# Pinning the norms, moving the choice of experts, and handing VectorE's work to ScalarE and GpSimd in the first third of a fused attention and mixture-of-experts block

## The chip, the cores and the metric

One core of a Trainium2 chip runs the whole program. The core has five engines, each with its own in-order instruction queue: TensorE (PE in the profile: matrix products and transposes), VectorE (DVE), ScalarE (ACT: activation functions and copies), GpSimd (POOL) and SyncE (SP, which mostly issues transfers). A queue starts its next instruction only when the one before it was started and its own waits are over, so what stands in front of what in a queue matters as much as how long it takes. The metric is the device time of one execution in microseconds (us). The kernel before has a median of 1208.85 us over five runs, from 1207.24 to 1213.85.

## The reference, cut to what matters

The input `x` holds 8 batches of 512 tokens with 512 features, in fp32.

```python
xn = layernorm(x)                                  # no weight, no bias
# attention: 16 heads of 32, chunks of 128 tokens, decayed linear attention
q = rotate(silu(xn @ Wq)); k = rotate(silu(xn @ Wk)); v = xn @ Wv
scores = einsum('bthd,bshd->bhts', q_c, k_c) * D   # D: decay mask of a chunk
o = scores @ v_c + (q_c * decay_q) @ S             # S: state carried over chunks
gate = xn @ Wg1 @ Wg2
o = group_rmsnorm(o * sigmoid(gate)) * norm_weight
s = o @ Wo
# mixture of experts: 16 experts of width 128, 4 chosen for each token, and a shared expert
logits = xn @ gate_w.T
weights, experts = top_k(softmax(logits), 4); weights /= weights.sum()
mixed = sum(weight_e * (silu(xn @ Wg[e]) * (xn @ Wu[e])) @ Wd[e])     # over the 4
shared = (silu(xn @ sWg) * (xn @ sWu)) @ sWd * sigmoid(xn @ shared_gate_w)
out = x + s * silu(mixed + shared)
```

## The kernel before, in words

The program is one long stretch of code for the core, with these stages (times in the span of the profiled execution):

- **0 to about 206 us.** The generator `first()` takes the 8 batches in turn. For each it makes the router's products (`route_1`: partial logits of all 512 tokens, four slices of the features side by side, copied to SBUF as `lT` by DVE, L311; `route_2`: their sum for each token, L323, then the four best experts, their weights and one-hot masks `oh` and `mask` on DVE), the shared expert (`share_1`: two products `pg` and `pu`, a SiLU on ACT, a product `h` on DVE, L366; `share_2`: four products `pys`, each of them taken out of PSUM and scaled by the shared gate `sg`, L380 on DVE or L382 on ACT, and stored to `sh_d`), the layer norm of the batch after next (`norm`: statistics L252 and L254 and centering L244 on DVE, the root of the variance on POOL, L256 and L258) and the transposes of the next batch (`turn`, L291, with ACT's copies L293). Each `yield` ends a piece. Beside these pieces runs the attention of batch 0: `value` (L576), `gate_1` to `gate_3` (L589, L598, L610), `enter` and `sequence` (rotated keys and queries L621, scores L679 and L700, outputs L718 and L722, root mean squares L729 to L754, projection L761). The function `along()` hands out 9 pieces of `first()` for every 5 of its steps.
- **206 to 246 us.** `sort()` gives each of the 16,384 pairs of token and expert a place in the list of its expert. Its long DVE steps are, for each of the four choices, a product `oa` (L445) and a sum over experts (L447), then small integer steps.
- **246 to 322 us.** `table()` turns the places into a table: which token stands at which row of which block of 128 rows. For each group of 16 lists, `make(i)` fills two one-hot arrays in fp16 on DVE, `place` (is the row equal to n: L512, then times the token's number: L514) and `block` (L517), in two halves of 8 lists each, and PE multiplies them into `pn` (L536). There are 8 groups. The generator is moved on by `between[0]`, which is called after every 4th of a product of `rotated` or `value`; beside it runs the attention of batch 1. Batch 1's own chain is on the same DVE.
- **340 to 740 us**: the expert blocks, each gathered, multiplied and stored. **745 to 1204 us**: the attention of batches 2 to 7 with the sum of everything. The change touches nothing there.

What sets the order: `on_pe()` chains every PE instruction behind the one traced before it, so PE's order is the order of the code. `behind(engine)` pins an instruction behind the last one traced for that engine. Everything without such a pin is placed by a scheduler that works out an order for each queue when the kernel is built. PSUM has 8 banks, given out in turn by tag: "a" has banks 0 to 3, "m" is bank 4, "d" is banks 5 and 6, "k" is bank 7. A matrix product must wait until the former holder of its bank has been read.

SP's queue holds, in the stretch of the sort and the table, the stores `s_d` of batch 0's projection (`spill`, L934), the loads `wexp` of 12 experts (L999, 768 KB each), stores of zeros (L1003) and the load of the transposed batch 2, `xT_2` (L558).

Of the kernel before, what the change touches and what calls it, by code (L numbers as in the profile page):

```python
# [11 lines left out]
F16 = mybir.dt.float16  # L12
# [7 lines left out]
P = 128  # L20
# [23 lines left out]
QUAD = 4  # L44
# [7 lines left out]
def shape_constants():  # L52

    f = np.float32
    c = {}
    lam = -(f(2.0) ** (f(-8.0) * (np.arange(H, dtype=f) + f(1.0)) / f(H))).astype(f)
    i = np.arange(C, dtype=f)
    diff = i[None, :] - i[:, None]
    dec = np.exp(lam[None, :, None] * np.maximum(diff, f(0.0))[:, None, :])
    c["dmask"] = np.where(diff[:, None, :] >= 0, dec, f(0.0))  # L60
    dq = np.exp(lam[:, None] * (i[None, :] + f(1.0)))
    c["dq"] = np.repeat(dq.reshape(G, HG, 1, C), HD, axis=2).reshape(G, P, C).transpose(1, 0, 2)
    c["dk"] = np.exp(lam[None, :] * (f(C) - f(1.0) - i[:, None]))
    lc = np.exp(lam * f(C))
    c["lamc"] = np.repeat(lc.reshape(G, HG, 1), HD, axis=2).reshape(G, P).T

    c["carry"] = np.tile(c["lamc"][:, :, None, None] * (np.arange(NC - 1) > 0), (1, 1, HD, 1))
    half = HD // 2
    theta = (f(BASE) ** (f(-2.0) * np.arange(half, dtype=f) / f(HD))).astype(f)
    ang = (np.arange(N, dtype=f)[None, :] * theta[:, None]).astype(f)  # L70
    c["cos"] = np.tile(np.cos(ang), (2 * HG, 1))
    c["sin"] = np.tile(np.concatenate([-np.sin(ang), np.sin(ang)], axis=0), (HG, 1))
    c["ident"] = np.eye(P)


    sel = np.zeros((P, H - HG + Q))
    exp = np.zeros((H, G, P))
    for g in range(G):
        for j in range(HG):
            sel[j * HD : (j + 1) * HD, H - HG + j] = 1.0 / HD  # L80
            exp[g * HG + j, g, j * HD : (j + 1) * HD] = 1.0
    c["sel"] = sel

    c["four"] = np.tile(np.eye(Q), (P // Q, P // Q))
    c["fold"] = np.tile(np.eye(Q)[:, :EA], (P // Q, 1))

    c["tri"] = np.triu(np.ones((P, P)), 1)
    c["iota_e"] = np.tile(np.arange(E), (P, 1))
    c["reset"] = np.tile((np.arange(NT) > 0)[None], (P, E)).reshape(P, E * NT)
    out = {k: np.ascontiguousarray(v.reshape(P, -1), dtype=f) for k, v in c.items()}  # L90
    out["exp"] = exp.reshape(H, D).astype(f)
    out["iota_b"] = (np.arange(P, dtype=f)[:, None] // Q * NBQ + np.arange(NBQ, dtype=f)).astype(f)

    out["whole"] = np.tile(np.arange(NB), (P, 1)).astype(np.float16)
    out["token"] = (
        np.arange(NT)[None, :] * P + np.arange(P)[:, None] - B * N // 2).astype(np.float16)
    return out


# [1 line left out]
def tile_block(ctx: ExitStack, tc: tile.TileContext, a: dict, out: bass.AP):  # L101
# [61 lines left out]
    iota_e = load(p1, "iota_e", [P, E])  # L163
    tri = load(p1, "tri", [P, P])
    reset = load(p1, "reset", [P, E * NT])
    token = load(const, "token", [P, NT], F16)
    whole = load(const, "whole", [P, NB], F16)
    iota_b = load(p1, "iota_b", [P, NBQ])
    ones = p1.tile([P, P], F32, tag="ones", name="ones")
# [62 lines left out]
    def norm(b):  # L232
        xs = xs_of[b]
        mv = p1.tile([P, NC, 2], F32, tag="mv", name=f"mv_{b}", bufs=2)
        rstd = p1.tile([P, NC], F32, tag="rstd", name=f"rstd_{b}", bufs=2)
        tiles = [slice(t, t + 1) for t in range(NC)] if b == 0 else [slice(0, NC)]

        def stand(engine):
            return behind(engine) if b < 2 else nullcontext()

        def center(ts):
            for t in range(ts.start, ts.stop):
                with stand(DVE):
                    nc.vector.tensor_scalar(  # L244
                        xs[:, t, :], xs[:, t, :], mv[:, t, 0:1], rstd[:, t : t + 1],
                        ALU.subtract, ALU.mult)

        for i, ts in enumerate(tiles):
            for t in range(ts.start, ts.stop):
                st = p1.tile([P, 6], F32, tag="st", name=f"st_{b}_{t}", bufs=4)  # L250
                with stand(DVE):
                    nc.vector.bn_stats(st, xs[:, t, :])  # L252
                with stand(DVE):
                    nc.vector.bn_aggr(mv[:, t, :], st)  # L254
            with stand(POOL):
                nc.gpsimd.tensor_scalar(rstd[:, ts], mv[:, ts, 1], LN_EPS, None, ALU.add)  # L256
            with stand(POOL):
                nc.gpsimd.tensor_tensor(  # L258
                    rstd[:, ts], rstd[:, ts],
                    root.to_broadcast([P, ts.stop - ts.start]), ALU.pow)  # L260
            if i:
                center(tiles[i - 1])
        center(tiles[-1])
        nc.sync.dma_start(
            xn_d[b * N : (b + 1) * N, :D].rearrange("(t p) d -> p t d", p=P),
            xs[:, :, : D // 2].bitcast(U16))
# [47 lines left out]
    def route_2(b):  # L314
# [9 lines left out]
        sg = p1.tile([P, NC], F32, tag="sg", name=f"sg_{b}", bufs=2)  # L324
        nc.scalar.activation(sg, lg[:, :, E], AF.Sigmoid)
        sg_of[b] = sg
        mx = p1.tile([P, NC, 8], F32, tag="mx", name=f"mx_{b}", bufs=2)
        ix = p1.tile([P, NC, 8], U32, tag="ix", name=f"ix_{b}", bufs=2)
        for t in range(NC):
# [39 lines left out]
    def share_2(b):  # L369
        h, sg = h1_of.pop(b), sg_of.pop(b)  # L370
        xT1_of.pop(b)
        for t in range(NC):
            sh = p1.tile([P, D], F32, tag="sh1", name=f"sh1_{b}_{t}", bufs=6)
            py = bank("dmaa"[t], f"pys_{b}_{t}")
            with on_pe():
                nc.tensor.matmul(
                    py, lhsT=h[:, t * P : (t + 1) * P], rhs=sw[:, KC * 2 * F :],
                    start=True, stop=True)
            if t % 2:
                nc.vector.tensor_scalar(sh, py, sg[:, t : t + 1], None, ALU.mult)  # L380
            else:
                nc.scalar.activation(sh, py, AF.Copy, scale=sg[:, t : t + 1])  # L382
            nc.sync.dma_start(sh_d[b][t * P : (t + 1) * P, :], sh)


    def sort():
# [54 lines left out]
        pos = p1.tile([P, TOPK, NT], F32, tag="pos", name="pos")  # L441
        bl = p1.tile([P, 2, TOPK, NT], I32, tag="bl", name="bl")
        for r in range(TOPK):
            with behind(DVE):
                nc.vector.tensor_tensor(oa[:, r], oh[:, r], at, ALU.mult)  # L445
            with behind(DVE):
                nc.vector.tensor_reduce(  # L447
                    pos[:, r], oa[:, r].rearrange("p e t -> p t e"), axis=AX.X, op=ALU.add)
            with behind(DVE):
                nc.vector.tensor_copy(posi[:, r], pos[:, r])  # L450
            with behind(DVE):
                nc.vector.tensor_scalar(bl[:, 0, r], posi[:, r], P - 1, None, ALU.bitwise_and)
            with behind(DVE):
                nc.vector.tensor_scalar(bl[:, 1, r], posi[:, r], 7, None, ALU.logical_shift_right)
            with behind(DVE):
                nc.vector.tensor_copy(
                    sp.rearrange("p w (r t) -> p w r t", t=NT)[:, :, r], bl[:, :, r])
            yield
# [16 lines left out]
    def table(room):  # L475
# [16 lines left out]
        free[0] = WE * LATE  # L492
        homes.append((part(quads, P, QUAD), part(quads, NB, QUAD)))
        count = part(NB, QUAD)
        acc = room[:, free[0] // 2 :][:, :NB]
        nc.scalar.copy(count, whole.unsqueeze(2).to_broadcast([P, NB, QUAD]))

# [4 lines left out]
        def make(i):  # L502
            place, block = homes[i // GROUP % 2]
            for u in range(0, quads, 2):
                us = slice(u, u + 2)
                lists = slice(i + u * QUAD, i + (u + 2) * QUAD)
                first = lists.start % NT

                def counts(n):
                    return count[:, :n].unsqueeze(1).to_broadcast([P, 2, n, QUAD])  # L510

                nc.vector.tensor_tensor(  # L512
                    place[:, us], counts(P), rows(sp[:, 0, lists], P), ALU.is_equal)
                nc.vector.tensor_tensor(  # L514
                    place[:, us], place[:, us], rows(token[:, first : first + 2 * QUAD], P),
                    ALU.mult)
                nc.vector.tensor_tensor(  # L517
                    block[:, us], counts(NB), rows(sp[:, 1, lists], NB), ALU.is_equal)

        make(0)  # L520
        for _ in range(KC + 1):
            yield
        for i in range(0, TOPK * NT, GROUP):
            if i + GROUP < TOPK * NT:
                make(i + GROUP)
            else:
                for e in range(E - LATE, E - LATE // 2):
                    nc.sync.dma_start(wexp[:, e, :], a["experts"][:, e, :])
# [4 lines left out]
            for some in ((0, 5), (5, 10), (10, GROUP)):  # L533
                with on_pe():
                    for j in range(*some):
                        nc.tensor.matmul(  # L536
                            pn[:, :NB], lhsT=place[:, j // QUAD, :, j % QUAD],
                            rhs=block[:, j // QUAD, :, j % QUAD], start=(j == 0),
                            stop=(j == GROUP - 1))
                if some[1] == GROUP:  # L540
                    if i:
                        nc.vector.tensor_tensor(acc, acc, pn[:, :NB], ALU.add)
# [394 lines left out]
    def first():  # L937

        for b in range(B):
            if 0 < b < B - 1:  # L940
                halves(b + 1)
            route_1(b)
            yield
            share_1(b)
            yield
# [8 lines left out]
            yield  # L954
            share_2(b)
            yield
        next(sorting)

    sorting = sort()
# [20 lines left out]

    for t in range(NC):
        value(0, t)
        along()
    gate_1(0)
    gate_2(0)
    gate_3(0)
    along()
    enter(0, along)
    sequence(0, along, spill, also=lambda: next(sorting, None))
# [324 lines left out]
```

## Time and profile before

| | us |
|---|---|
| median of five runs | 1208.85 (1207.24 to 1213.85) |
| the profiled execution | 1205.38 |
| its span | 1203.6 |
| PE busy in the span | 1160.5 (96%) |
| DVE busy | 751.9 (62%) |
| POOL busy | 437.9 (36%) |
| ACT busy | 407.2 (34%) |

The profiled execution is 3.47 us faster than the median and faster than each of the five runs. All durations below are from it. The mean clock that TensorE was granted is 0.993 of full speed.

How to read it: PE is busy for 96% of the span, so time is gained only where PE stops, where its clock is lowered, or where it does less. The 43 us in which PE stands still are 23.5 us before 340 us and less behind; the list of PE's waits says which engine and which line ended each of them. Shares of busy time of the other engines are averages over stages; what counts is whether DVE or ACT is the one that PE waits for in a given stretch.

### The profile page before, as it was taken

How to read it: one execution, taken by the hardware profiler on the slowest of the kernel's cores; microseconds unless marked ns; L12 is line 12 of the kernel's file. 1: busy time of each engine (PE TensorE's matmuls, PEld its weight loads, DVE VectorE, ACT ScalarE, POOL GpSimd, SP SyncE). 2: the span in 40 equal slices, each digit the busy share in tenths (PEclk: the TensorE clock that was granted, in tenths of full speed). 3: DMA queues.
4: the chain of work that ended last, by engine and by line, in shares of the span. 5: the costliest groups of instructions: out<-in, count | busy, mean ns of one | idle time of the engine just before them, and what ended most of it. 6: DMA issues, size and time to landing. Idle time of an engine off the chain costs nothing. (4 is left out here: it accounts for less than half of the span.)

```text
span 1203.6 us, 21260 instructions
## 1 busy us (share of the span) xinstructions
PE 1160.5 (96%) x7708; PEld 684.3 (57%) x7708; DVE 751.9 (62%) x1584; ACT 407.2 (34%) x767; POOL 437.9 (36%) x424
## 2 busy tenths in 40 slices
PE   6999999999999999999999999999999999999997
PEld 3435554446557777777777775545544545545453
DVE  6387554889414444444434444979879599598784
ACT  3343333320274444444444442141141411411420
POOL 3123002100213333333333331862876847858111
PEclk9999999989999999999999999999999999999999
DMA  9884231183458999989999996931845627544012
GB/s 325 286 296 166 102 136 71 25 315 117 146 150 212 224 233 229 227 229 231 229 213 234 223 222 186 344 119 56 271 130 182 206 87 252 146 125 145 18 39 68
DMA packets 163496, 217.16 MB, mean 180 GB/s; under 512 B 89792, under 2 KB 98880, under 8 KB 161472
## 3 DMA queue, kind: packets, MB, share of 16 engines
q1 hardware_dynamic: 141984, 143.88, 40.0%
q0 software_dynamic: 21120, 70.34, 21.1%
q10 hardware_dynamic: 288, 1.57, 0.4%
q8 instruction: 64, 1.05, 0.4%
q14 instruction: 40, 0.33, 0.1%
HBM read 125.55 MB, written 72.35 MB: 164 GB/s over the span
## 5 line engine op out<-in xcount | busy, mean ns | idle before, releaser
L1076 PE MATMUL pgu<-wexp,xt 128*128 x1088 | 257.6, 380 | 1.5 <-ACT xt L1057 1.2
L1076 PEld LDWEIGHTS pgu<-wexp,xt 128*128 128x128 f32 x1088 | 206.0, 190 | 88.6 <-issue 31.1
L1035 POOL DMA_INDIRECT xg<-xn_d,slot x79 | 74.6, 944 | 249.3 <-DVE y L1106 164.1
L1173 POOL DMA_INDIRECT yg<-y_d,posi x128 | 140.4, 1097 | 47.2 <-SPq L1140 19.6
L1081 DVE TENSOR_TENSOR slb<-slb,pgu 128x128 f32<-128x128 f32 x136 | 39.0, 287 | 189.6 <-ACT slb L1080 189.6
L1059 ACT COPY xt<-pl 128x512 uint16<-128x512 uint16 x136 | 104.3, 767 | 131.4 <-DMA pl<-xg 75.9
L1097 PE MATMUL py<-wexp,hT 128*128 x272 | 139.3, 594 | 0.1
L576 PE MATMUL pv<-wv,xT 128*128 128x512 f32 x256 | 119.9, 604 | 3.9 <-DVE sh L380 2.8
L621 PE MATMUL pk<-xT,wk 128*128 128x512 f32 x256 | 118.3, 603 | 1.7 <-DVEq L1140 1.7
L621 PE MATMUL pq<-xT,wq 128*128 128x512 f32 x256 | 117.4, 599 | 0.0
L761 PE MATMUL pw<-wo,on 128*128 128x512 f32 x224 | 102.3, 604 | 3.1 <-DVE m L1201 3.0
L1205 POOL TENSOR_TENSOR xo<-xo,m 128x512 f32<-128x512 f32 x30 | 43.2, 1440 | 152.1 <-DVE m L1201 142.3
L1035 POOL DMA_INDIRECT more<-xn_d,slot x57 | 53.6, 941 | 109.5 <-DVE y L1106 106.6
L700 DVE TENSOR_TENSOR sc<-ps,dmask 128x512 f32<-128x512 f32 x128 | 79.1, 676 | 0.8 <-PE ps L679 0.8
L576 PEld LDWEIGHTS pv<-wv,xT 128*128 128x128 f32 x256 | 45.7, 191 | 58.1 <-issue 51.3
L621 PEld LDWEIGHTS pq<-xT,wq 128*128 128x128 f32 x256 | 47.8, 193 | 52.8 <-issue 51.5
L1106 DVE TENSOR_SCALAR y<-py,xg 128x512 f32<-128x512 f32 x79 | 59.3, 750 | 29.2 <-PE py L1097 29.1
L621 PEld LDWEIGHTS pk<-xT,wk 128*128 128x128 f32 x256 | 46.1, 190 | 52.0 <-issue 49.6
L761 PEld LDWEIGHTS pw<-wo,on 128*128 128x128 f32 x224 | 41.8, 192 | 54.5 <-issue 47.0
L1080 ACT ACTIVATE slb<-pgu 128x128 f32<-128x128 f32 x136 | 37.8, 278 | 85.6 <-PE pgu L1076 85.3
L626 ACT ACTIVATE sk<-pk 128x512 f32<-128x512 f32 x32 | 19.1, 596 | 116.4 <-PE pk L621 107.6
L580 ACT COPY v<-pv 128x512 f32<-128x512 f32 x32 | 18.8, 589 | 108.3 <-PE pv L576 102.5
(169 smaller groups left out, 1765.1 us busy)
## 6 DMA issues: line engine op xcount, KB each, us to landing
y_d<-y SPq DMA_DIRECT2D x136, 256.0 KB, 3.0
wexp<-in_experts SPq DMA_DIRECT2D x14, 768.0 KB, 11.5
sh_d<-sh SPq DMA_DIRECT2D x32, 256.0 KB, 2.7
m<-sh_d SPq DMA_DIRECT2D x32, 256.0 KB, 4.6
xo<-in_x SPq DMA_DIRECT2D x32, 256.0 KB, 3.5
out<-xo SPq DMA_DIRECT2D x32, 256.0 KB, 2.1
x<-in_x SPq DMA_DIRECT2D x7, 1024.0 KB, 6.1
xT_d<-xT SPq DMA_DIRECT2D x7, 1024.0 KB, 5.4
```

The costliest lines, as they stand in the source:

```text
L576: nc.tensor.matmul(pv, lhsT=xT_of[b][:, k, t * P : (t + 1) * P], rhs=wv[:, k, :], start=(k == 0), stop=(k == KC - 1))
L621: nc.tensor.matmul(ps, lhsT=w[:, k, g * P : (g + 1) * P], rhs=xT_of[b][:, k, :], start=(k == 0), stop=(k == KC - 1))
L700: nc.vector.tensor_tensor(s, pss[j].rearrange("p (c t) -> p c t", t=C), dmask[:, g * HG + j].unsqueeze(1).to_broadcast([P, NC, C]), ALU.mult)
L761: nc.tensor.matmul(pw, lhsT=on_of[b][:, g, t * P : (t + 1) * P], rhs=wo[:, g, :], start=(g == 0), stop=(g == G - 1))
L1035: nc.gpsimd.indirect_dma_start(out=row(i), out_offset=None, in_=xn_d, in_offset=bass.IndirectOffsetOnAxis(ap=slot[:, i : i + 1], axis=0))
L1059: nc.scalar.copy(xt[:, KP:, :].bitcast(U16).rearrange("p k (t h) -> p h k t", h=2), turned(i).rearrange("p (h k) t -> p h k t", h=2))
L1076: nc.tensor.matmul(pg[:, : 2 * F], lhsT=xt[:, k, :], rhs=wflat[:, bass.ds(off + k * 2 * F, 2 * F)], start=(k == 0), stop=(k == KC - 1))
L1081: nc.vector.tensor_tensor(sl, sl, pg[:, F : 2 * F], ALU.mult)
L1097: nc.tensor.matmul(py, lhsT=hT_of.pop(i), rhs=wflat[:, bass.ds(off_of.pop(i) + KC * 2 * F, D)], start=True, stop=True)
L1106: gone.append(nc.vector.tensor_scalar(y, py, row(i).bitcast(F32)[:, bass.ds(at, 1)], None, ALU.mult).ins)
L1173: nc.gpsimd.indirect_dma_start(out=yg, out_offset=None, in_=y_d, in_offset=bass.IndirectOffsetOnAxis(ap=posi[:, r, g : g + 1], axis=0))
L1205: nc.gpsimd.tensor_tensor(xo, xo, m, ALU.add)
```

## The change

The change has seven parts.

1. `norm(b)`: all its instructions on DVE and POOL are pinned behind the last one traced, for every batch; before, only for batches 0 and 1. In DVE's queue the norm of batch b+2 then stands right behind the product `h` of `share_1(b)`.
2. The choice of experts leaves `route_2(b)` and becomes `route_3(b)`, which is called behind the next batch's `route_1`.
3. `share_2` takes its four banks as "dama" in place of "dmaa", and all four results are taken out of PSUM by ACT (L380's 16 DVE instructions in this phase become 16 more of ACT's).
4. The gates of batch 0 are no longer three in a row behind the four `value` products, but one behind each of the last three.
5. The four products `oa` of the sort run on POOL in place of DVE.
6. In the table, the numbers of the tokens are multiplied into the second 8 of each 16 lists by ACT, in 64 activations of 128x128 with a scale from a column of `token`, in place of 8 of the 16 DVE products L514. `token` is loaded in fp32, and a copy in fp16 is made on ACT for the other half.
7. `make(0)` stands behind a first `yield`.

```diff
@@ norm
-        def stand(engine):
-            return behind(engine) if b < 2 else nullcontext()
-
         def center(ts):
             for t in range(ts.start, ts.stop):
-                with stand(DVE):
+                with behind(DVE):
                     nc.vector.tensor_scalar(
...
-                with stand(DVE):
+                with behind(DVE):
                     nc.vector.bn_stats(st, xs[:, t, :])
-                with stand(DVE):
+                with behind(DVE):
                     nc.vector.bn_aggr(mv[:, t, :], st)
-            with stand(POOL):
+            with behind(POOL):
                 nc.gpsimd.tensor_scalar(rstd[:, ts], mv[:, ts, 1], LN_EPS, None, ALU.add)
-            with stand(POOL):
+            with behind(POOL):
                 nc.gpsimd.tensor_tensor(
@@ route_2, and first()
         sg_of[b] = sg
+        lg_of[b] = lg
+
+    def route_3(b):
+        lg = lg_of.pop(b)
         mx = p1.tile([P, NC, 8], F32, tag="mx", name=f"mx_{b}", bufs=2)
...
             route_1(b)
+            if b:
+                route_3(b - 1)
             yield
             share_1(b)
...
+        route_3(B - 1)
         next(sorting)
@@ share_2
-            py = bank("dmaa"[t], f"pys_{b}_{t}")
+            py = bank("dama"[t], f"pys_{b}_{t}")
...
-            if t % 2:
-                nc.vector.tensor_scalar(sh, py, sg[:, t : t + 1], None, ALU.mult)
-            else:
-                nc.scalar.activation(sh, py, AF.Copy, scale=sg[:, t : t + 1])
+            nc.scalar.activation(sh, py, AF.Copy, scale=sg[:, t : t + 1])
@@ the attention of batch 0
     for t in range(NC):
         value(0, t)
+        if t:
+            (gate_1, gate_2, gate_3)[t - 1](0)
         along()
-    gate_1(0)
-    gate_2(0)
-    gate_3(0)
     along()
@@ sort
-            with behind(DVE):
-                nc.vector.tensor_tensor(oa[:, r], oh[:, r], at, ALU.mult)
+            nc.gpsimd.tensor_tensor(oa[:, r], oh[:, r], at, ALU.mult)
@@ table
+        half_token = half[:, free[0] : free[0] + NT]
+        free[0] += NT
+        nc.scalar.copy(half_token, token)
...
                 nc.vector.tensor_tensor(
                     place[:, us], counts(P), rows(sp[:, 0, lists], P), ALU.is_equal)
-                nc.vector.tensor_tensor(
-                    place[:, us], place[:, us], rows(token[:, first : first + 2 * QUAD], P),
-                    ALU.mult)
+                if u == 0:
+                    nc.vector.tensor_tensor(
+                        place[:, us], place[:, us], rows(half_token[:, lists.start % NT :][
+                            :, : 2 * QUAD], P), ALU.mult)
...
+        def number(i, some):
+            place = homes[i // GROUP % 2][0]
+            for j in range(max(some[0], GROUP // 2), some[1]):
+                row = place[:, j // QUAD, :, j % QUAD]
+                t = (i + j) % NT
+                nc.scalar.activation(row, row, AF.Copy, scale=token[:, t : t + 1])
+
+        yield
         make(0)
-        for _ in range(KC + 1):
+        for j in range(0, GROUP, QUAD):
+            number(0, (j, j + QUAD))
             yield
         for i in range(0, TOPK * NT, GROUP):
-            if i + GROUP < TOPK * NT:
+            more = i + GROUP < TOPK * NT
+            if more:
                 make(i + GROUP)
...
+                if more:
+                    number(i + GROUP, some)
```

## The prediction

> **What bounds the kernel now.** I read the page's first two parts, then the list of PE's waits up to 340 us (the change ends there), then windows with the clock, then single waits in the timeline. Engine shares first:
>
> ```profile
> PE 1160.5 (96%) x7708; PEld 684.3 (57%) x7708; DVE 751.9 (62%) x1584; ACT 407.2 (34%) x767; POOL 437.9 (36%) x424
> ...
> PEclk9999999989999999999999999999999999999999
> ```
>
> PE is the bound, and the change removes no PE instruction, so it can win only idle time and lowered clock. The waits of PE up to 340 us (engine, line, releaser: total, times, longest):
>
> ```profile
> PE psT L291 <- DMA ident<-in_ident: 6.4, 1, 6.4
> PE pv L576 <- DVE sh L380: 2.8, 2, 2.1
> PE p L610 <- DVE sc L700: 2.5, 1, 2.5
> PE ps L679 <- DVE sc L700: 1.5, 1, 1.5
> PE ps L679 <- DVE sh L380: 1.3, 1, 1.3
> PE pv L576 <- DMA xT<-xT_d: 1.1, 1, 1.1
> PE pn L536 <- DVE sc L700: 0.9, 1, 0.9
> ```
>
> After the start's 6.4 us, most are ended by DVE (L380, L700). The waits sum to 23.5 us, 17.1 without the start. Windows show a second cost, the clock (the column after POOL):
>
> ```profile
> 30.00:34.00 4.00, 4.00 (x12) 1.52 (x16) 0.86 (x3) 0.34 (x1) 0.00 (x0) 1.00 1.05 370
> 111.30:114.70 3.40, 3.40 (x15) 2.06 (x15) 3.19 (x8) 0.00 (x0) 0.00 (x0) 0.50 0.12 45
> 254.70:258.10 3.40, 3.40 (x9) 1.66 (x9) 3.40 (x7) 2.01 (x4) 0.00 (x0) 0.50 1.01 421
> ```
>
> Behind the 1.27 us wait at 110.2 the clock was 0.50 for 3.4 us, behind the 2.54 us wait at 254 for 6.8 us; half of each is lost, 1.7 and 3.4 us. Behind 2.11 us at 29.9, and behind waits of 0.95 to 1.46 elsewhere, it stayed 1.00. The wait with the dearest tail in the timeline (start, us, engine, line, ..., idle before):
>
> ```profile
> 253.24 1.28 DVE L700 TENSOR_TENSOR sc<-ps,dmask 128x512 f32<-128x512 f32 x2
> ...
> 253.98 0.69 PE L610 MATMUL p<-g,wg 32*128 32x512 f32 x1 [2.54 <-DVE sc L700]
> ```
>
> The gate's products need the PSUM banks that DVE's `sc` empties, and `sc` stands behind ten table instructions, which stand behind the sort. DVE is busy 18.60 of the 20 us from 240, ACT 6.04.
>
> The trace belongs to an execution of 1205.38 us, span 1203.6; the median is 3.47 higher. I add the sum to both, as the edits lie in stages that every execution has.
>
> **The change part by part** (negative is faster).
>
> *Shared parts on ACT, banks "dama".* 16 L380 of 742 ns leave DVE (11.9 us), 16 of 679 ns join ACT (10.9 us), which was busy 3 to 4 tenths there. The bank that `value` waits for at 29.93 (m) is now freed by an ACT instruction that runs before PE comes (last `pys` ends 27.81): −2.05, bounds −2.11 and −1.4 (0.68 of one more ACT result in front). At 79.28 the 0.35 wait goes; at 203.2 the third result on ACT ends when DVE's did: 0. At 133.1 the 0.81 wait for `on` goes, but bank 6 now waits for a query's SiLU behind the norm: +0.2 (−0.8 to +1.2).
>
> *Gates.* Before, 66.05 to 71.53 us with waits of 0.71, 0.68 and 0.77: 5.48 us. Apart they cost PE 0.99 + 0.95 + some 2.4 of products. But `gate_3` now follows `value(0,3)`, and one of its banks is held by a shared part whose reader stands behind the copy of `v` (0.59), a table load (1.28) and sigmoids (0.60 each): a wait of 1.6. Sum 5.97: +0.5, bounds −2.2 (all waits covered) and +2.2 (clock tail of 1.7).
>
> *Norms pinned, choice moved.* For batches 2 to 7, DVE makes 4 L252 (0.67), 4 L254 (0.17), waits for POOL's L256 and L258 (0.23 + 1.04; the round trip at 115.5 left DVE idle 1.47) and centers 4 L244 (0.68), some 6.5 us in one block in front of a key's rotation or the next `lT`. The choice (max, index, one-hots: small, 0.16 to 0.22 us each, about 20) moves behind the next `lT`, which helps the router's next product. POOL's queue: the halves (0.70 each) stand behind the root as before; SP's: the stores `xn_d`, `sh_d` only change places. What waits is `ps` at 110.2: without the `sh` in front, but with a norm, `lT` of batch 4 ends at 111.3 instead of 110.76, and `ps` ends where it did. I take 0, one clock window as before; bounds −3.0 (wait and tail gone) and +2.3 (longer wait, two windows). The other five norms have PE's pieces of the shared expert and transposes beside them: 0; their cover is the second rival.
>
> *`oa` on POOL.* DVE loses four L445; its instructions start 0.61 to 0.72 apart, 2.75 together. POOL was idle from 215 to 241. Its nearest rows are L391 with 1.37 (first `wt`), 2.31 at worst, so the four fill 225.4 to 231.7. The first sum L447 ran at 230.0 and needs its product at 226.8: covered. Against it: while POOL's 2.31 us product ran, small DVE instructions stretched:
>
> ```profile
> 212.39 1.17 DVE L416 TENSOR_SCALAR ci<-incl 128x16 int32<-128x16 f32 x1
> 213.59 0.17 DVE L418 TENSOR_SCALAR ci<-ci 128x16 int32<-128x16 int32 x1
> 213.80 1.13 DVE L421 CAST nb<-ci 128x16 f32<-128x16 int32 x1
> ```
>
> 1.17 and 1.13 where 0.17 is usual, so two such losses of 1.0 cost up to 2.0, and one or none is possible: I take 1.25 lost, bounds 0 and 6.5 (DVE blocked through all four at 2.31, 9.24, less 2.75). The Trainium skill (SBUF — State Buffer, "two separate sides") says that a DVE instruction with two SBUF inputs and a reading GpSimd instruction lock each other out entirely. The rows agree for conversions; by the rule the nine rotations and products beside `oa` would each wait out what is left of a POOL instruction, by estimate 5 to 6 us, and the sum would be 4 us worse.
>
> *Table.* ACT gets one 128x32 copy (about 0.2, on the path before `make(0)`), and 64 activations. L1080's 128x128 takes 0.278; the scale by a pointer costs about 0.09 on 128x512 (0.679 against 0.585): 0.28 to 0.37 each, 18 to 24 us, on an ACT that was idle some 53 us from 246 to 310 (busy 6.04, 2.48 and 1.77 in the windows of 20 us from 240). In front of the first `sc` stand ten wide DVE instructions as before. So `sc` comes 2.75 − 1.25 − 0.2 = 1.3, say 1.2 us earlier, the wait of 2.54 shrinks to about 1.35, and of waits between 1.27 and 1.67 only one in four had a slow clock behind it: I take both windows as gone: −1.2 − 3.4 = −4.6. Bounds −5.9 and, with the `oa` bound, +6.5. ACT's `so_3` (246.7 before) now stands behind nine activations that wait for DVE, to about 252, and `sk` behind seven more, to 255.2; their banks are needed again only from 261 and 265. SP's queue holds nine `wexp` loads behind the store of `so_3`; see the third rival.
>
> Later: `pn` at 271.6 +0.15 (a 0.74 L517 where a 0.68 L514 stood). From 289 to 301.8 DVE was the bound:
>
> ```profile
> 302.50 1.15 PE L679 MATMUL ps<-qT,kT 32*128 32x128 f32 x8 [1.46 <-DVE sc L700]
> ```
>
> There four L514 and an L517 are gone (about 3 us); DVE then waits for `pn` itself, and `sc` comes 1.1 earlier: −1.1, bounds −1.46 and 0. `sq` of the last key waits for eight activations, but ends before DVE takes it: 0 (up to +0.9).
>
> Sum: −2.05 −0.35 +0.2 +0.5 +0 −4.6 +0.15 −1.1 = −7.25. Profiled execution 1198.1, median 1208.85 − 7.25 = **1201.6**.
>
> **The rivals.**
> *The slow clock stays* behind the wait at 254, or comes behind `gate_3`. For: 1.27 us was enough at 110. Against: 2.11 was not at 29.9. It gives back 3.4 (1205.0), with both 5.1 (1206.7). The Trainium skill (TensorE: Matmul & The Clock Gate, "What's actually happening") says that the clock falls after an idle window of about 3.4 us; the row of 1.27 us contradicts it, and by the rule no wait here would slow the clock.
>
> *The norms become the bound* (slower). In DVE's queue a whole norm with POOL's answer stands in front of the rotation, and PE has no cover. Each would cost the 1.47 round trip and 1.7 of clock, 3.2, up to 6.5 + 1.7 = 8.2; six make 1201.6 + 19 = 1220.8 at the low price, three at 5.6 make 1218.4. It decides when more than two of six norms cost 3.2 (7.25 / 3.2). For: at 116.9 DVE stood 1.47 idle for it already. Against: DVE was free for 17 to 42% of the windows of 20 us from 20, 60, 100 and 120, and PE never waited for L244 after the start.
>
> *A transfer ends the wait anyway.* `xT_2` landed at 285.51, 1.10 after PE wanted it. It was issued when PE's last read of batch 1 allowed (6.7 us of SP's wait), 2.4 after the last zeros landed (278.34). If the store of `so_3` holds the `wexp` loads 4 us, those 2.4 are used up; the landing comes up to 2.5 late: 1204.1. Against: the first load starts 2.6 earlier.
>
> *Nothing moved* is excluded for `sh` and `oa`, whose rows change engine.
>
> **How the numbers follow.** Chances: the forecast 0.58, clock 0.20, norms 0.15, transfer 0.07. The forecast's own range, from its bounds added loosely, is 1197 to 1204.5. 0.5% is 6.04 us, about what a measurement of this kernel can tell from no change: 1202.8 and 1214.9. Faster: 0.8 of the forecast, 0.46. Slower: 0.8 of the norms, 0.12. Same: the rest, 0.42. The range 1197 to 1210.5 leaves out the norms at their likely prices and a little of the forecast below.
>
> **What would show it.** Right: no wait at 30; the wait for L700 at about 1.4 near 250 with clock 1.00 behind it; `sc` near 297 with under 0.5; L447 not waiting for POOL. Wrong: PE waiting for a rotation or `lT` behind L244; POOL's `oa` above 2 us with DVE's instructions beside it at 1 us or more; half clock behind the gates; a wait for `xT` over 1.1.

## The result and the profile after

The changed kernel has a median of 1203.13 us (1199.45 to 1211.01, 23 runs), the kernel before, on the same chips, 1209.5 us (1204.22 to 1220.0, 44 runs). The ratio is 0.9944 with a 95% interval of 0.9928 to 0.996: 0.56% faster, 6.4 us between the medians. The forecast was 7.25 us less and 1201.6. The size was near. Of the steps below it some were right, one came out for a wrong reason, and the half clock behind the sort went only by half.

The profiled execution of the changed kernel took 1204.27 us, 1.1 less than the profiled one before (1205.38), and 1.1 *more* than its own median. So most of the gain is not to be seen by laying these two profiles side by side. The waits of PE up to 340 us, from the list of waits (engine, line, releaser: total, times, longest), show what became of the list before; line numbers have moved by a few (old L576 is L588, L610 is L622, L679 is L691, L700 is L712, L380 and L382 are L380, L311 is L308):

```profile
PE psT L288 <- DMA ident<-in_ident: 6.3, 1, 6.3
PE ps L691 <- DVE lT L308: 2.5, 2, 2.3
PE p L622 <- ACT on L625: 1.5, 1, 1.5
PE pv L588 <- DMA xT<-xT_d: 1.2, 1, 1.2
PE pn L546 <- DVE sc L712: 1.0, 1, 1.0
PE pys L377 <- ACT sq L638: 1.0, 1, 1.0
PE p L622 <- DVE sc L712: 0.9, 1, 0.9
```

The 2.1 us for a shared part at 30 us is gone; the 2.5 us for `sc` in front of the gate's products is 0.9. The router's copy `lT` now ends a wait of 2.3 us at the place where `sh` ended one of 1.3, and 1.5 us for a bank of `gate_3` are new. All waits over 0.1 us up to 340 us sum to 20.0 us where they were 23.6.

The windows (last column but two is PE's clock; before it the busy time of PE, its weight loads, DVE, ACT and POOL) show where the clock was at half in this execution:

```profile
62.30:65.70 3.40, 3.40 (x11) 0.70 (x10) 0.60 (x1) 2.80 (x5) 0.00 (x0) 0.50 1.06 240
113.50:116.90 3.40, 3.40 (x6) 1.51 (x5) 3.40 (x13) 0.00 (x0) 0.00 (x0) 0.50 0.69 253
256.90:260.30 3.40, 3.40 (x7) 1.71 (x7) 2.72 (x5) 2.63 (x5) 0.00 (x0) 0.50 1.02 423
```

The first of these lasts 6.8 us in the trace's clock records, the others 3.4. That is 13.6 us at half clock ahead of the end, as much as in the profile before, at other places. Compare the same work in both: at 172 us PE was 1.9 us *later* than before (173.91 against 172.03), at 254 us 0.4 later, at 302 us 1.15 earlier (301.35 against 302.50), and so to the end.

### The profile page after: what moved, and what is told of

Its sections match the earlier page's. It is cut to its first block, busy times and chain, and to the rows that moved or that the text cites. A ratio compares the mean times of both kernels' runs of the same rounds, so it can differ in the third digit from the quotient of the medians.

```text
span 1202.4 us, 21355 instructions
## 1 busy us (share of the span) xinstructions
PE 1162.3 (97%) x7708; PEld 683.1 (57%) x7708; DVE 735.5 (61%) x1556; ACT 443.0 (37%) x852; POOL 444.4 (37%) x428
## 3 DMA queue, kind: packets, MB, share of 16 engines
q8 instruction: 64, 1.05, 0.4%
## 5 line engine op out<-in xcount | busy, mean ns | idle before, releaser
L588 PE MATMUL pv<-wv,xT 128*128 128x512 f32 x256 | 119.9, 604 | 2.1 <-DMA xT<-xT_d 1.2
L712 DVE TENSOR_TENSOR sc<-ps,dmask 128x512 f32<-128x512 f32 x128 | 79.2, 676 | 0.6 <-PE ps L691 0.6
L588 PEld LDWEIGHTS pv<-wv,xT 128*128 128x128 f32 x256 | 45.7, 191 | 56.1 <-issue 51.4
L1120 DVE TENSOR_SCALAR y<-py,more 128x512 f32<-128x512 f32 x57 | 42.7, 750 | 20.0 <-PE py L1111 20.0
```

The costliest lines, as they stand in the source:

```text
L588: nc.tensor.matmul(pv, lhsT=xT_of[b][:, k, t * P : (t + 1) * P], rhs=wv[:, k, :], start=(k == 0), stop=(k == KC - 1))
L712: nc.vector.tensor_tensor(s, pss[j].rearrange("p (c t) -> p c t", t=C), dmask[:, g * HG + j].unsqueeze(1).to_broadcast([P, NC, C]), ALU.mult)
L1120: gone.append(nc.vector.tensor_scalar(y, py, row(i).bitcast(F32)[:, bass.ds(at, 1)], None, ALU.mult).ins)
```

## The experiments

Each kernel below was timed in rounds beside the kernel before, and each has one profile. "Waits" are those of PE up to 340 us.

### The changed kernel again

No edit.

> The changed kernel once more, unedited, as the yardstick for the other runs beside it. Theory (part of the time is chance: half-clock stretches of TensorE that come behind some waits in some executions): the waits of PE come at the same places and sizes as in the first profile (1.5 us behind the gates, 2.3 us for lT near 112, 0.9 near 254, within 0.1 us), but the places of the half clock differ from it, and the time is 1200 to 1207. Rival (the half clock belongs to certain waits): the same three stretches behind 62, 113 and 257 us, 6.8, 3.4 and 3.4 us long.

Median 1203.73 us, ratio 0.9954 (0.9929 to 0.998); profiled execution 1200.05 us. Windows of its profile:

```profile
60.40:63.80 3.40, 3.11 (x13) 0.96 (x14) 0.69 (x1) 3.15 (x6) 0.01 (x1) 1.00 0.90 236
107.60:111.00 3.40, 2.69 (x25) 2.28 (x26) 3.40 (x18) 0.25 (x1) 0.00 (x0) 0.50 1.05 387
254.30:257.70 3.40, 3.40 (x8) 1.58 (x7) 2.77 (x5) 2.71 (x5) 0.00 (x0) 0.50 1.00 417
```

The waits over 0.3 us are the same to 0.02 us from 8 to 210 us (1.52 for `gate_3`, 2.32 for `lT`), but no half clock follows the gates: the window from 60.4 has 1.00. At `sc` the wait was 1.37 in place of 0.93, outside the 0.1 us that I had given. Two executions of one program, nearly the same waits, 4.2 us apart. In the main the first theory holds: behind a wait like that of the gates half clock can come in one execution and stay away in the next.

### The gates in a row

```diff
         value(0, t)
-        if t:
-            (gate_1, gate_2, gate_3)[t - 1](0)
         along()
+    gate_1(0)
+    gate_2(0)
+    gate_3(0)
     along()
```

> The gates of batch 0 in a row again, all else as changed. Theory (the new place costs: one wait of 1.5 us for a bank behind a table load, against three waits of 0.7 us whose sum is 2.1, and a clock tail of 3.4 us that shorter waits seldom have): PE is through the gates some 0.5 us earlier by waits alone, and the median is 1 to 4 us below the changed kernel's. Rival (the new place gains, as fewer waits make up for the products): 1 to 2 us above it.

Median 1201.35 us, ratio 0.9929 (0.9902 to 0.9956), against 0.9954 for the unedited kernel beside it. The three waits are back (0.71, 0.68, 0.77), the 1.52 is gone, and no half clock followed them in the profile. The medians lie 2.4 us apart in the direction of the first theory, but the intervals overlap widely: the new place of the gates is not a gain that these runs can show. The two profiles, this one and that of the kernel run again, say more, since neither has half clock there. This one reaches the products `plT` in front of the gates 1.91 us earlier (29.37 against 31.28, a lead from the start of the program) and the products `pl` behind them 1.89 us earlier (69.64 against 71.53). So waits and products together cost the same in both places, not 0.5 us less in a row. What differs is the half clock: it starts within 2.6 us behind the 1.52 us wait in four of the seven profiles that have that wait, and behind the three short waits in none of five. That the new place is a loss is likely by this, and open by the medians.

### Only gate_3 moved

```diff
         value(0, t)
-        if t:
-            (gate_1, gate_2, gate_3)[t - 1](0)
+        if 0 < t < 3:
+            (gate_1, gate_2)[t - 1](0)
         along()
+    gate_3(0)
     along()
```

> Only gate_3 is moved, behind the pieces that follow the last value product; gate_1 and gate_2 stay where the change put them. Theory (the 1.5 us wait is the copy of v, a table load and sigmoids between the product and the free bank): with some 15 us of other products between, PE's wait at the gates is under 0.3 us and no half clock follows; the median is 2 to 4 us below the changed kernel's. Rival (the wait only moves, since ACT's sigmoids then stand in front of other banks' readers): a wait of 0.7 us or more for ACT within 10 us behind it, and the median within 1 us.

Median 1201.28 us, ratio 0.9914 (0.9885 to 0.9943). The list of its waits has no wait for `gate_3`, but one that was not there:

```profile
PE pys L377 <- ACT sk L638: 1.3, 1, 1.3
```

It stands at 78 us, with a 0.67 us wait for the sigmoids at 69 us: so the rival was right about the waits (the sigmoids stand in front of other readers on ACT), while the median is 2.4 us under the unedited one, within the overlap of the intervals.

### The norms left to the scheduler

```diff
+        def stand(engine):
+            return behind(engine) if b < 2 else nullcontext()
...
-                with behind(DVE):
+                with stand(DVE):
                     nc.vector.bn_stats(st, xs[:, t, :])
```

(and so at each of the norm's instructions.)

> The norms of batches 2 to 7 are left to the scheduler again, all else as changed. Theory (the pinned norm stands in front of a rotation and lT and makes the 2.3 us wait near 112): that wait falls to under 1.3 us, no other grows, and the median is 1 to 2.5 us below the changed kernel's. Rival (pinning is a gain: a free norm is placed later and PE waits for centering or transposes): new waits of PE for L244's successor or ACT's xT, and the median 1 us or more above.

Median 1206.18 us, ratio 0.9966 (0.9941 to 0.9991). I was wrong on both of the waits. The one at `lT` grew from 2.32 to 3.58, and the one at 30 us, which the forecast had put down to DVE as the reader, came back with ScalarE as the reader. Timeline of PE in this kernel (start, us, engine, line, operation, idle before):

```profile
27.80 1.02 PE L380 MATMUL pys<-sw,h 128*128 128x512 f32 x2
30.80 1.69 PE L591 MATMUL pv<-wv,xT 128*128 128x512 f32 x2 [1.98 <-ACT sh L383]
```

In the changed kernel the same place has no gap:

```profile
27.55 1.45 PE L377 MATMUL pys<-sw,h 128*128 128x512 f32 x3
28.92 3.27 PE L588 MATMUL pv<-wv,xT 128*128 128x512 f32 x7
```

DVE's timeline there tells why. Before:

```profile
24.38 1.92 DVE L244 TENSOR_SCALAR x<-x,mv,rstd 128x512 f32<-128x512 f32 x4 [1.48 <-POOL rstd L258]
26.21 0.22 DVE L323 COPY lg<-pl 128x68 f32<-128x68 f32 x1
```

and in the changed kernel:

```profile
25.51 0.23 DVE L320 COPY lg<-pl 128x68 f32<-128x68 f32 x1 [0.39 <-PE pl L316]
25.66 0.17 DVE L251 BATCH_NORM_AGGREGATE mv<-st 128x2 f32<-128x6 f32 x1
```

Before, the free norm was run early, and its wait for POOL (1.48) and four centerings (1.92) stood in front of the logits `lg`, 1.9 us behind the end of their product. The shared gate `sg`, the exponentials and every shared part need `lg`. ScalarE's timeline before has the rest of the chain:

```profile
26.46 0.21 ACT L325 ACTIVATE sg<-lg 128x4 f32<-128x4 f32 x1 [0.89 <-DVE lg L323]
26.69 1.28 ACT L338 ACT_TABLE_LOAD   x1
...
28.10 1.25 ACT L382 ACTIVATE sh<-pys,sg 128x512 f32<-128x512 f32 x2
```

The gate waited 0.89 us for `lg`, and then a table load and an exponential of the choice stood in front of the first shared part. In the changed kernel, and in the kernel with the norms alone pinned, the first shared part follows the gate at once (26.77 and 27.00; 24.07 and 24.32), and the exponential comes behind. A pinned norm starts later, its statistics leave room for `lg` as soon as the product is there (0.39 us of idle), and its centering comes behind.

### The shared parts as before

```diff
-            py = bank("dama"[t], f"pys_{b}_{t}")
+            py = bank("dmaa"[t], f"pys_{b}_{t}")
...
-            nc.scalar.activation(sh, py, AF.Copy, scale=sg[:, t : t + 1])
+            if t % 2:
+                nc.vector.tensor_scalar(sh, py, sg[:, t : t + 1], None, ALU.mult)
+            else:
+                nc.scalar.activation(sh, py, AF.Copy, scale=sg[:, t : t + 1])
```

> The shared parts as before (banks dmaa, two of four taken out by VectorE), all else as changed. Theory of the forecast (the 2.11 us wait at 30 us goes because the bank is now emptied by ScalarE): the wait for a shared part comes back near 29 us with 1.4 to 2.1 us, and the median is 1 to 4 us above the changed kernel's. Rival (the pinned norm, which leaves VectorE free in time, took the wait away; in the run with free norms a wait of 1.98 us for a shared part on ScalarE stood there): no wait over 0.5 us near 29 us, and the median within 1.5 us.

Median 1207.31 us, ratio 0.9986 (0.9958 to 1.0013). There is no wait at 30 us, so the rival's reading of that place is right. But the median is 3.6 us above that of the unedited kernel (timed beside other runs of the kernel before, so only roughly), and the rows say where waits grew: at `ps`, 2.65 us near 113 and 0.69 near 143.

```profile
PE ps L694 <- DVE sh L381: 3.3, 2, 2.7
```

So the wait that the 16 instructions make longer is that at `ps`, behind the pinned norm, not one at 30 us. What it is worth is open: all waits sum to 20.5 us here, no more than in the changed kernel (20.0 and 20.9), and the intervals overlap.

### The norms alone, on the kernel before

```diff
-            return behind(engine) if b < 2 else nullcontext()
+            return behind(engine)
```

> The kernel before with one part of the change alone: the norms of all batches pinned. Theory formed after the runs on the shared parts (the wait at 29.93 us was not the reader's engine: a free norm was run early, its centering and POOL's answer kept VectorE from the logits lg until 26.2 us, and all behind them was late): the wait near 30 us falls from 2.1 to under 1.0 us. Rival (the choice of experts in front of the shared part is what was late, and it is still there): 1.3 us or more remain. The median lies within 3 us of the kernel before in both.

Median 1217.1 us, ratio 1.005 (1.0015 to 1.0085): slower than the kernel before. The wait at 30 us is gone here too, with DVE still reading two of the shared parts. In exchange:

```profile
PE ps L679 <- DVE sh L380: 4.4, 1, 4.4
PE pys L376 <- DVE on L722: 2.9, 1, 2.9
```

These were 1.3 and 0.8 before. The median is 5.5 us above that of the kernel before, more than the 3 that I had allowed. The clock records have 10.2 us at half clock from 106.6 us on in this profile, and 34.1 ahead of the end, where the profile before has 13.6. The pinned block in front of the rotations is what the second rival of the forecast described. It is dear when it is alone.

### The shared parts alone, on the kernel before

```diff
-            py = bank("dmaa"[t], f"pys_{b}_{t}")
+            py = bank("dama"[t], f"pys_{b}_{t}")
...
-            if t % 2:
-                nc.vector.tensor_scalar(sh, py, sg[:, t : t + 1], None, ALU.mult)
-            else:
-                nc.scalar.activation(sh, py, AF.Copy, scale=sg[:, t : t + 1])
+            nc.scalar.activation(sh, py, AF.Copy, scale=sg[:, t : t + 1])
```

> The kernel before with the shared parts alone changed (banks dama, all four on ScalarE). By the forecast's step the 2.1 us wait near 30 us is gone and the median 2 to 4 us lower. By the theory formed since (ScalarE is as late as VectorE there, since its gate sg and the exponentials wait for the logits) a wait of 1.5 us or more for a shared part remains near 30 us, the one near 110 us becomes a wait for lT or stays, and the median is within 3 us.

Median 1204.82 us, ratio 0.9962 (0.9927 to 0.9996). The wait at 30 us is not removed, it is longer, with ScalarE as its releaser:

```profile
PE pv L573 <- ACT sh L379: 3.5, 1, 3.5
```

The forecast's step "the bank is now freed by ScalarE, −2.05" is refuted. The waits elsewhere got shorter (1.27 to 0.86 at `ps`, now for `lT`; the 0.69 at 203 us gone), and the median fell by some 6.7 us against the kernel before beside it, which is more than I expected of it; the interval, from 0.5 to 8.8 us, does not say how much of that is real. It is not the sum of the waits, which rose from 23.6 to 25.4 us; the granted clock is 0.992 in the mean over these runs and 0.990 in those beside them, by estimate some 3 us of the span.

### The choice of experts back in route_2

```diff
             route_1(b)
-            if b:
-                route_3(b - 1)
             yield
...
             route_2(b)
+            route_3(b)
             yield
...
-        route_3(B - 1)
         next(sorting)
```

> The choice of experts back in route_2, all else as changed. Theory (the choice and its exponential, with a table load of 1.28 us on ScalarE, stand in front of the shared parts again): a wait of 0.5 to 2 us for a shared part comes back near 29 us, and the median is 1 to 4 us above the changed kernel's. Rival (with pinned norms the logits are early enough for both): no such wait, and the median within 1.5 us.

Median 1208.56 us, ratio 0.9989 (0.9963 to 1.0015). No wait at 29 us, so that part of my theory was wrong, but the median is 4.8 us above that of the unedited kernel (timed beside other runs of the kernel before, and with an interval that overlaps). The list of waits has the place:

```profile
PE pys L377 <- DVE on L734: 2.9, 1, 2.9
```

The 2.93 us near 135 us is the one that the norms alone bring. In the changed kernel it is 0.96. So the choice, moved behind `lT`, takes back what the pinned norm costs at 135 us, and the shared parts on ScalarE take back a part of what it costs near 110.

### The sort's products on VectorE

```diff
-            nc.gpsimd.tensor_tensor(oa[:, r], oh[:, r], at, ALU.mult)
+            with behind(DVE):
+                nc.vector.tensor_tensor(oa[:, r], oh[:, r], at, ALU.mult)
```

> The four products oa on VectorE again, all else as changed. Theory (VectorE's queue is what the wait near 253 us is made of, and the four cost it 2.75 us, less what GpSimd's lock takes): the wait of 0.9 to 1.4 us becomes 2.3 to 3.6 us, and with the clock tail the median is 1.5 to 5 us above the changed kernel's. Rival (the lock and the later start take back as much): the wait stays under 1.6 us and the median within 1 us.

Median 1207.34 us, ratio 0.9972 (0.9947 to 0.9996). Timeline of PE in this kernel and then in the changed one:

```profile
253.64 2.41 PE L623 MATMUL p<-g,wg 32*128 32x512 f32 x5 [2.75 <-DVE sc L713]
```

```profile
254.40 1.89 PE L622 MATMUL p<-g,wg 32*128 32x512 f32 x5 [0.93 <-DVE sc L712]
```

The wait is 1.4 to 1.8 us longer with the products on DVE (0.93 and 1.37 in the two profiles of the changed kernel), and the half clock behind it lasts 6.8 us where both of those had 3.4. The theory holds.

### The table on VectorE

```diff
-                if u == 0:
-                    nc.vector.tensor_tensor(
-                        place[:, us], place[:, us], rows(half_token[:, lists.start % NT :][
-                            :, : 2 * QUAD], P), ALU.mult)
+                nc.vector.tensor_tensor(
+                    place[:, us], place[:, us], rows(token[:, first : first + 2 * QUAD], P),
+                    ALU.mult)
...
-        yield
         make(0)
-        for j in range(0, GROUP, QUAD):
-            number(0, (j, j + QUAD))
+        for _ in range(KC + 1):
             yield
```

(with the number activations and the fp16 copy left out, and `token` in fp16.)

> The table as before (all products with the token numbers on VectorE, no first yield), all else as changed. Theory: the wait near 299 us for the last scores grows from 0.8 to 1.3 to 1.6 us, the one near 252 us changes by under 0.3 us since ten wide VectorE instructions stand in front of the scores in both, and the median is 0.5 to 2 us above the changed kernel's. Rival (the ScalarE numbers are a cost, as they stand in front of a key's SiLU and a store): the waits near 252 and 281 us get shorter, and the median is 1 us or more below.

Median 1208.28 us, ratio 0.9981 (0.9957 to 1.0006). The wait for the last scores is 1.45 us where the changed kernel has 0.79, as expected. The one near 252 is 1.94, 0.6 to 1.0 longer, which I had not expected. My premise was wrong: DVE's timelines show twelve wide table instructions in front of `sc` here (from 243.83 us on), ten in the changed kernel (from 246.72) and ten in the kernel before. The median is 4.6 us above that of the unedited kernel, more than the 0.5 to 2 expected, with intervals that overlap. The rival is out: neither of the waits that it named got shorter (1.94 near 252, 1.34 near 285), so the activations save waits and do not cost them.

### The router's copy on ScalarE

```diff
-        nc.vector.tensor_copy(lT, plT)
+        with behind(ACT):
+            nc.scalar.copy(lT, plT)
```

(and gate_3 late, as above.)

> The changed kernel with gate_3 late, and the router's copy lT moved from VectorE to ScalarE, pinned behind ScalarE's last shared part. Theory (the 2.3 us wait near 108 us is lT behind a norm and a rotation in VectorE's queue, and its bank is all that PE lacks): that wait falls under 0.6 us, no new one over 1 us comes in the first 200 us, and the median is 2 to 5 us below the changed kernel's, 1 to 3 below that with gate_3 late alone. Rival (what PE lacks comes next, since VectorE's rotation is as late for the scores): a wait of 1.5 us or more at the same place with another releaser, and the median as with gate_3 late alone.

Median 1201.75 us, ratio 0.9935 (0.9907 to 0.9963). The wait at `lT` fell from 2.32 to 0.86, more than the 0.6 I gave, and a wait of 1.85 for `sk` came near 78 us, 0.6 more than with gate_3 late alone. Another of 1.29 for a shared part came near 59 us; I had said that none over 1 us would come. The waits sum to 21.5 us, against 20.8 with gate_3 late alone, and the time is that of gate_3 late within the intervals. The theory was right on the cause of the wait and wrong on its worth: both new waits are ended by ScalarE, where the router's copies now stand in front of other work.

### The candidate

```diff
+    gate_1(0)
+    gate_2(0)
+    gate_3(0)
...
-        nc.vector.tensor_copy(lT, plT)
+        with behind(ACT):
+            nc.scalar.copy(lT, plT)
```

(and no gates behind the `value` products.)

> A candidate: the changed kernel with the gates in a row and the router's copy lT on ScalarE. The wait of 1.3 to 1.9 us near 78 us, which both kernels with gate_3 late have, does not come up with the gates in a row; the wait near 108 us is 0.9 us as with lT on ScalarE. Sum of PE's waits up to 340 us 1 to 2 us below that with gate_3 late and lT on ScalarE (21.5), and the median 1200 to 1202. If the waits of the gates are as dear as the one at 78, the two candidates are equal within 1.5 us.

Median 1200.39 us (1195.29 to 1204.95), ratio 0.9921 (0.9895 to 0.9948). Its longest waits behind the start:

```profile
PE pg L362 <- ACT sh L381: 1.3, 1, 1.3
PE pv L589 <- DMA xT<-xT_d: 1.1, 1, 1.1
PE pn L547 <- DVE sc L713: 1.0, 1, 1.0
```

No wait over 1.3 us is left up to 340 us but the start, and in its profile only one half-clock stretch of 3.4 us falls there. The sum of waits is 20.8, 0.7 below that with gate_3 late and `lT` on ScalarE, not the 1 to 2 I expected. It has the lowest median here and is clearly faster than the kernel before; against the changed kernel (0.9954 and 0.9944) its interval overlaps, so that it is better is likely and not shown. If it is, the clock is the reason and not the sum of the waits, which is 20.0 and 20.9 in the changed kernel: the granted clock is 0.9947 in the mean over these runs and 0.9920 over those of the changed kernel, by estimate 3.2 us of the span.

## Why the prediction was right, and where its steps were not

**Shared parts, −2.05 at 30 us: the size came out, the cause was wrong.** I took the reader's engine for the cause, since the list named `sh` on DVE as what ended the wait. Shown: with that part alone the wait is 3.49 us on ScalarE; with the pinned norms alone it is gone, with DVE still reading. What was late was the logits `lg` behind a norm that ran early. That another part of the change took this wait away, and with the forecast size, was luck. The −0.35 at 79 us came, +0.2 at 133 us came as 0.96 against 0.81.

**Norms, 0: near in the changed kernel, but it hung on the other parts.** In the changed kernel the waits at the two places are 2.32 and 0.96 us where 1.27 and 0.81 stood. The longer wait is not all lost: PE was 1.49 us later than before at the products `plT` in front of it (108.32 against 106.83) and 1.23 later at `pg` behind it (113.64 against 112.41). Some 0.6 us of this is half clock, which before began in front of `pg` (at 111.29) and here behind it (at 113.53), so by estimate the place cost 0.3 us and not 1.05. The half clock behind it lasted 3.4 us in one profile, as forecast, and 6.8 in the other. Alone, the pinned norms make the kernel 0.5% slower, with 4.35 and 2.93 us at the two places. I had listed this as a rival for slower with 0.15, and priced it at 3.2 to 8.2 for each of six norms; the two places grew by 5.2 us together. What I missed is how much of the gain of parts 2 and 3 is spent on covering part 1, and that part 1 in turn removes the wait at 30 us. Undone one at a time, in ratio: choice 0.9989, shared parts 0.9986, table 0.9981, `oa` 0.9972, norms 0.9966, and the other way the gates 0.9929, against 0.9944 and 0.9954 for the whole. Each has an interval of some 0.0026 to either side, so no one of them is well known; but the differences sum to twice the whole gain or more, which speaks against adding the parts up as I did.

**Gates, +0.5 with a wait of 1.6: the wait was 1.52.** The timelines of ACT and of PE show its three pieces in the order forecast:

```profile
59.15 0.58 ACT L592 COPY v<-pv 128x512 f32<-128x512 f32 x1 [2.97 <-PE pv L588]
59.75 1.28 ACT L625 ACT_TABLE_LOAD   x1
61.04 1.08 ACT L625 ACTIVATE on<-p 128x512 f32<-128x512 f32 x2
```

```profile
61.69 0.69 PE L622 MATMUL p<-g,wg 32*128 32x512 f32 x1 [1.52 <-ACT on L625]
```

The cost is not +0.5: by the two profiles compared under the gates in a row, waits and products together came to nothing. The clock tail behind the wait, which I kept for the range, came with 6.8 us in one execution and not in the other.

**`oa` on POOL, −2.75 + 1.25: right, with less lost than allowed.** In the changed kernel's timeline:

```profile
227.37 3.39 POOL L442 TENSOR_TENSOR oa<-oh,at 128x512 f32<-128x512 f32 x2 [11.92 <-DVE at L436]
227.81 0.68 DVE L766 TENSOR_TENSOR on<-on,pb 128x512 f32<-128x512 f32 x1
...
228.41 1.19 DVE L644 TENSOR_TENSOR qT<-qT,swq 128x512 f32<-128x512 f32 x1
```

One rotation took 1.19 in place of 0.68, and a cast 0.38 in place of 0.18: 0.7 us in all. The Trainium skill (SBUF — State Buffer, "two separate sides") speaks of two SBUF inputs; the rotation agrees: L644 reads two and was held, L766 reads one of its inputs from PSUM and kept its 0.68. The cast here, and the conversions of 1.17 and 1.13 us that I took as agreeing, read one input, so two inputs are not their reason, and these runs do not show what is. My 5 to 6 us by that rule counted instructions that read PSUM or did not fall into POOL's 5.9 us.

**Table: the wait went as forecast, the clock did not.** The wait for `sc` shrank by 1.6 and 1.2 us (forecast 1.2), but not by `oa` alone: with the table back on VectorE, which I had priced at nothing here, it is 0.6 to 1.0 longer. But I took all of the half clock behind it as gone (−3.4), because of four waits between 1.27 and 1.67 only one had one. In both profiles of the changed kernel 3.4 us remain, and in eight of the nine profiles here with a wait of 0.8 to 1.4 us at this place half clock of 3.4 or 6.8 us starts within 3.4 us of its end. So −1.7, not −3.4, is the price in these profiles, and the place, or what runs behind it, matters beside the wait's length. The last scores gained 0.67 where I said 1.1. The activations took 0.34 each (0.28 to 0.37 forecast), and no wait of PE names them.

**The transfer of batch 2** ends a wait of 1.2 to 1.4 us, 1.10 before: the third rival gave 0.1 to 0.3 us, not 2.5.

**Signs.** Of the signs of being wrong that the forecast named, three came: PE waited for `lT` behind a norm, half clock followed the gates in one of two profiles, and the wait for `xT` was over 1.1. Of those of being right, the clock of 1.00 behind the wait near 250 and the wait under 0.5 for the last `sc` did not come.

**Why the total still came out.** Without the clock, my steps are −2.05 −0.35 +0.2 +0.5 −1.2 +0.15 −1.1 = −3.85. The sums of the waits give −3.6 and −2.7 (23.6 to 20.0 and 20.9). PE's own progress says much the same: PE goes on with the last scores at 302.50 us before and at 298.98 in the profile run again, 3.5 us earlier with as much half clock behind it (10.2 us). The medians fell 6.4. The rest lies in how much half clock an average execution has, and each run's granted clock shows it: the mean is 0.9903 over the 20 runs of the kernel before beside the kernel run again, 0.9920 over the 9 runs of that, and 0.9920 over 25 runs of the result. Times the span, by estimate, that is 2.1 us less lost to the clock, with a standard error of about 1, and 3.9 of the 6.0 us between the means are left for everything else. So both halves came out near: forecast −3.85 and measured −3.9 without the clock, −3.4 and −2.1 by the clock. But I had put all of the clock's half behind the sort, where only −1.7 of it is seen in these profiles. That fewer and shorter waits make fewer half-clock stretches is argued from the places below; where the rest of it falls is not shown. The single profile before was a lucky one, 4.1 us under the median of its 44 runs; executions of the changed kernel take 1199.7 to 1203.8 us where their mean granted clock is 0.994 (seven of them), and 1204.9 to 1211.0 where it is 0.988 or 0.989 (four).

## What to carry to other kernels

The releaser that a wait names is the last link of a chain; before moving that instruction to another engine, follow its inputs back in its queue, here to a norm that ran too early. Pins, moves and engine changes in one queue pay for each other, so price them together, or undo them one by one. A single profile carries chance in it where the clock falls behind waits: compare waits between profiles, and times and granted clocks only between many runs. A longer wait is not yet lost time: compare when PE reaches the same product behind it.

## What was not expected of the hardware

- The places of half clock differ between executions of one program with equal waits: behind the same 1.52 us wait 6.8 us in one and none in the other, in steps of 3.4 us. The two executions were 4.2 us apart.
- Half clock came 1.8 to 3.4 us behind waits as short as 0.9 us (0.93 at 254.4, half clock from 256.9).
- The place counts beside the length. Over the 14 profiles here, half clock came with the wait for `lT` or `sh` near 110 us in all eleven where it is 1.27 us or longer and in none of the three where it is 0.86; with the wait for `sc` near 254 in all but the one of 0.84. That fits the candidate, whose 0.86 near 108 us has none.
- The four products of 128x512 took GpSimd 5.90 us, the first two of them 3.39, where DVE takes 0.68 for one.
